# Typed graph convolution with residual and normalisation on one core: rank product behind the counts, register loads a step ahead, squares on ScalarE, edge codes on TensorE

## The chip, the cores and the metric

The kernel runs on one core of one Trainium2 chip. The metric is device time in microseconds of one execution; a profiled execution also gives a trace of every engine. Engines are named as the profile names them: PE (TensorE), PEld (its weight loads), DVE (VectorE), ACT (ScalarE), POOL (GpSimd) and SP (SyncE, which issues DMAs). A name with a q, such as DVEq, is the engine's sequencer.

## The reference

There are 12,500 nodes with 128 features and 400,000 edges, sorted by their target `dst`. Every edge is of one of two types.

```
Xs      = x[src]
m_data  = Xs @ W_data.T + b_data
m_ctrl  = Xs @ W_control.T + b_control
msg     = where(edge_type == 0, m_data, m_ctrl)
agg     = segment_sum(msg, dst, 12500)
h       = x + relu(agg + x @ W_self.T + b_self)
out     = (h - mean(h)) / sqrt(var(h) + 1e-5)      # over the 128 features
```

## The kernel before, in words

Sums commute with the products by W, so the kernel sums the rows of x by target and type first, and multiplies the sums by the weights after that. x is held as three bf16 parts of an fp32 number (`x3` in SBUF, `rows3` in DRAM), and one-hot matrices on TensorE pick and add rows.

The 400,000 edges are 25 groups (`g`, 125 chunks of 128 edges). A group has five windows; of each, 5 chunks are "p" chunks, whose rows come by an indirect DMA on POOL (`fetch`, tile `msg`, one gather per chunk), and 20 are "e" chunks, whose rows are picked from SBUF by matmuls (`pick`, tile `got`, cast by ACT to `emsg`). In two groups of three the fifth window consists of p chunks alone. That leaves 109 e windows, and the main loop has one step `w` for each. A step is five units `t` on PE: picks of some cells into `got`, then additions (`add`, into the bank `sums`, with the one-hot `esel` that DVE makes) of the cells picked one unit earlier. The last additions of a step are done in unit 0 of the next one, by `end`, which then has DVE add the bank to `acc` at an offset that a register holds (`accumulate`; `place_of` loads the register on DVE's queue, line 854). The p chunks go through banks of the same pair (`sums`, two buffers, `psel`), with counts in `cnt`.

Which edges go to which cell of a step is worked out by a chain on DVE, two steps ahead: `O` (the 0/1 matrix of edges and cells, made three steps ahead), `tens` and `fold_few` (its counts), `before` (four counting products on PE, line 634), `ahead` (a reduction of their result, line 642), `product` (O by ahead, line 648), `fold`, `eighth`, `found`, `rank`, `rank_matrix` (rm), `values` (rv). From rv PE makes the table (`put`, tile side, line 726), ACT casts it (`cell`), SP stores it and reads it back spread over all partitions (`pick`), and DVE compares it (`pick_matrix`). Edges beyond the table's room go a side way: `over` (a search for the 8 largest keys), `om_all` and line 574 on PE.

Two more jobs run beside the steps. `prep(g)` turns a group's indices and types into codes on the right partitions, by transposes on PE. `finish_batch`, 25 times, takes up to four tiles of finished sums, multiplies by the weights (line 1095), adds x, and normalises (`norm`, `write`).

PSUM holds one bank `side` (a single buffer, shared by put, the side way, prep, finish and before), two banks `sums`, and `got`. Each engine works its list strictly in order. The order is set by hand: every piece of work has a place between 0 and 1 in the step, `merged` sorts by it, and `in_turn` ties DVE's chain together; a scheduler then sets the final lists.

Of the kernel before, what the change touches and what calls it, by code (L numbers as in the profile page):

```python
# [8 lines left out]
FP = mybir.dt.float32  # L9
# [10 lines left out]
P = 128  # L20
# [188 lines left out]
def short_path(ctx, tc, const, ident, eps, wT, brow, bad, x, src, dst, etype, ws, bs, out):  # L209
# [269 lines left out]
    def prep(g):  # L479

        s, d, t = raw.pop(g)
        v = 0 if sets(g) == NE else 1
        width = bounds_of[:GC, v, 0:1]
        sf = pre.tile([GC, P], FP, name="sf", bufs=1)
        rel = pre.tile([GC, 2, P], BF, name="rel", bufs=1)
        code = pre.tile([GC, 2, P], FP, name="code_r", bufs=1)
        kind = pre.tile([GC, P], FP, name="kind_r", bufs=1)
        idx = pre.tile([P, GC], I32, name="idx_g", bufs=3)
# [6 lines left out]
        def rows():  # L495
            near = near_of(g, d)
            for k in range(2):
                nc.vector.tensor_scalar(rel[:, k], d, near[k], None, op0=OP.subtract)
            nc.vector.tensor_single_scalar(kind, t, 0.0, op=OP.not_equal)
            nc.vector.scalar_tensor_tensor(code[:, 1], kind, width, rel[:, 1], op0=OP.mult, op1=OP.add)  # L500
            nc.vector.scalar_tensor_tensor(code[:, 0], kind, float(PW), rel[:, 0], op0=OP.mult, op1=OP.add)
            for j, op in enumerate((OP.max, OP.min)):
                nc.vector.tensor_tensor(worst[:GC, v, j], worst[:GC, v, j], rel, op=op)

        def turn():
            ps = side()
            for k, each in enumerate((sf, code[:, 1], code[:, 0])):
                nc.tensor.transpose(ps[:, k * P:k * P + GC], each, ident[:GC, :GC])
# [86 lines left out]
    def give_slots(w):  # L595
# [32 lines left out]

        def before():
            s["ahead"] = side()  # L630
            cols = s["ahead"][:, :2 * NCELL].rearrange("p (k j) -> p k j", k=2)
            for a in range(4):
                cells = slice(a * NQ, (a + 1) * NQ)
                nc.tensor.matmul(  # L634
                    cols[:, :, cells], ltri[:, a, :], s["few"][:, 3 * CQ:3 * CQ + 2, cells],
                    start=(a == 0), stop=True, skip_group_check=True,
                )

        def ahead(prev=None):
            s["ahead_b"] = two.tile([P, NCELL], BF, name="ahead")  # L640
            with nc.allow_low_precision(reason="whole numbers; those over 256 need not be exact"), after(prev):
                return nc.vector.tensor_reduce(  # L642
                    s["ahead_b"], s["ahead"][:, :2 * NCELL].rearrange("p (k j) -> p j k", k=2), AX.X, OP.add
                )
# [201 lines left out]
    def acc_rows(g, a, b):  # L846
        begin_acc(g)
        return acc[g][:, a:b, :]

    def place_of(g, i):  # L850

        parts_in[g] = parts_in.get(g, 0) + 1
        with tc.issue_after(added[-2].ins) if len(added) > 1 else ExitStack():
            return nc.vector.value_load(raw["place"][0:1, g, i:i + 1], min_val=0, max_val=R - WMAX)  # L854
# [96 lines left out]

    def picked(w, tiled, ending, before):

# [46 lines left out]
        def unit(t):  # L1000
# [10 lines left out]
            if t == 0:  # L1011
                choose(0, 10)
                gates = ending() or [gate]
            while counts:
# [46 lines left out]
    def finish_batch(g, tiles):  # L1061
# [37 lines left out]
        def norm():  # L1099
            h = s["h"] = fp.tile([P, 4, D], FP, name="h")  # L1100
            st = fp.tile([P, 4, 6], FP, name="st")
            mv = s["mv"] = fp.tile([P, 4, 2], FP, name="mv")
            for i, (_, _, rows) in enumerate(tiles):
                nc.vector.scalar_tensor_tensor(
                    h[:rows, i, :], s["ph"][:rows, i * D:(i + 1) * D], 0.0, s["xs"][:rows, i, :], op0=OP.max, op1=OP.add
                )
            for i, (_, _, rows) in enumerate(tiles):
                if rows < full:
                    nc.vector.memset(mv[:, i, :], 1.0)
                nc.vector.bn_stats(st[:rows, i, :], h[:rows, i, :])  # L1110
                nc.vector.bn_aggr(mv[:rows, i, :], st[:rows, i, :])

        def write():
            h, mv = s["h"], s["mv"]
            rows = full
            sd = fp.tile([P, 4], FP, name="sd")
            nc.scalar.activation(sd[:rows, :k], mv[:rows, :k, 1], AF.Sqrt, bias=eps[:rows])
            rs = fp.tile([P, 4], FP, name="rs")
            nc.vector.reciprocal(rs[:rows, :k], sd[:rows, :k])
            for i, (n, _, r) in enumerate(tiles):  # L1120
                nc.vector.tensor_scalar(
                    h[:r, i, :], h[:r, i, :], mv[:r, i, 0:1], rs[:r, i:i + 1], op0=OP.subtract, op1=OP.mult
                )
# [95 lines left out]

    def ending():  # L1220
        pass

# [6 lines left out]
    for w in range(pairs):  # L1229
# [8 lines left out]
        if i == 3 and g + 2 < NG:  # L1238
            load(g + 2)
        tiled, begin, chain, first = {}, [], {}, None  # L1240
        if w + 2 < pairs:
            tiled, first, chain = slots[w + 2]["tiled"], slots[w + 2]["before"], slots[w + 2]["chain"]
            begin = [(0.58, slots[w + 2]["over"])]
        elif w + 2 == pairs:
            tiled, begin = last_spares()
            first = begin.pop(0)[1]
        if w + 3 < pairs:
            more += [(0.503, lambda: begin_slots(w + 3))]
# [4 lines left out]
        units, ending, (second, third) = picked(w, tiled, ending, first)  # L1253
# [4 lines left out]
        order = [  # L1258
            (0.305, second), (0.31, chain.get("ahead")), (0.33, chain.get("product")), (0.34, chain.get("half")),
            (0.36, third), (0.38, chain.get("fourth")), (0.51, chain.get("eighth")),  # L1260
            (0.52, chain.get("found")), (0.53, started("same")), (0.54, chain.get("rank")),
            (0.55, chain.get("matrix")), (0.56, chain.get("key")), (0.57, chain.get("values")),
            (0.6, (lambda prev: pick_matrix(w + 1, prev)) if w + 1 < pairs else None),
            (0.62, started("blocks")), (0.64, started("tens")), (0.66, started("fold5")),
            (0.67, started("fold2")), (0.68, started("fold1")),
        ]
# [163 lines left out]
```

## Time and profile before

| | us |
|---|---|
| median of 3 runs | 1719.48 (1718.93 to 1721.28) |
| the profiled execution's own time | 1719.45 |
| its span | 1717.7 |
| busy: DVE | 1577.5 |
| busy: PE | 1554.5 |
| busy: ACT | 1229.1 |
| busy: POOL | 1217.5 |

Busy times are unions of instruction times, without register, semaphore and DMA-issuing instructions. The granted clock of PE was 0.996. An engine's idle time is put down to what it waited for last; "issue" stands where the profile shows nothing to wait for. In rows of groups, the numbers behind the bar are the busy time, the mean duration in ns, and the idle time ahead of the group with what ended it.

### The profile page before, as it was taken

The page shows a single profiled execution, that of the slowest core. Times are in us where ns is not written, and L with a number is a line of the kernel's source. Part 1 is how long each engine was busy: PE and PEld are TensorE (multiplying, and loading weights), DVE is VectorE, ACT ScalarE, POOL GpSimd, SP SyncE. Part 2 cuts the span into 40 slices and gives each one's busy share as a digit, 9 for nine tenths or more (in the row PEclk, how much of TensorE's full clock was granted, in tenths as well). Part 3 has the DMA queues.
Part 4 walks back from the last instruction along what each step waited for, and adds up shares of the span by engine and source line. Part 5 has one row for each costly group of instructions (what it writes and reads, how often), then busy time and mean ns, then how long its engine had stood idle before and what let it go on. Part 6 is the DMA issues. An engine that isn't in the chain of part 4 may idle for free.

```text
span 1717.7 us, 67684 instructions
## 1 busy us (share of the span) xinstructions
PE 1554.5 (90%) x27966; PEld 1225.1 (71%) x27966; DVE 1577.5 (92%) x4078; ACT 1229.1 (72%) x2056; POOL 1217.5 (71%) x1022
## 2 busy tenths in 40 slices
PE   0699999899999999899899999999999999999998
PEld 0477777777777777777777777777777777777776
DVE  9799999999999999999999999999999999999994
ACT  7677767677767777677676777677686777677774
POOL 1377767777776777667777777677777787787682
PEclk9999999999999999999999999999999999999999
DMA  7944444444454444444444454444444454444442
GB/s 227 269 136 134 148 129 148 135 150 135 133 153 133 146 151 132 148 130 140 143 140 135 137 157 132 148 152 132 142 133 150 139 156 130 128 148 129 141 125 59
DMA packets 147605, 246.05 MB, mean 143 GB/s; under 512 B 35565, under 2 KB 114264, under 8 KB 147288
## 3 DMA queue, kind: packets, MB, share of 16 engines
q1 hardware_dynamic: 99128, 142.50, 24.9%
q0 software_dynamic: 48160, 99.14, 21.8%
q8 instruction: 221, 3.62, 0.8%
q14 instruction: 96, 0.79, 0.1%
HBM read 224.04 MB, written 17.52 MB: 141 GB/s over the span
## 4 chain that ended last, share of the span: by engine, by line
DVE 66%; PE 19%; issue 7%; ACT 3%; DVEq 3%; DMA 1%; SPq 0%; ACTq 0%
DVE esel L541 9%; PE sums L803 8%; DVE O L541 6%; DVE prod L656 6%; PE got L974 6%; DVE pick L790 5%; DVE prod L648 5%; DVE rv L713 4%; DVE psel L541 3%; DVE prod L627 3%; DVE prod L622 3%; DVE rm L541 2%; DVEq L854 2%; DVE found L666 2%; DVE prod L612 2%
## 5 line engine op out<-in xcount | busy, mean ns | idle before, releaser
L871 POOL DMA_INDIRECT msg<-rows,idx_g x945 | 1140.2, 1207 | 365.3 <-PE got L974 121.0
L988 ACT CAST emsg<-got 128x768 bf16<-128x768 f32 x1090 | 965.5, 929 | 305.0 <-PE got L974 291.2
L803 PE MATMUL sums<-esel,emsg 128*128 128x172 bf16 x7848 | 685.9, 238 | 7.9 <-DVE acc L860 7.8
L803 PEld LDWEIGHTS <-emsg 128*128 128x128 bf16 x7848 | 571.2, 98 | 118.8 <-issue 111.7
L974 PE MATMUL got<-x,pick 128*32 128x384 bf16 x10682 | 578.9, 330 | 9.8 <-ACT emsg L988 3.8
L974 PEld LDWEIGHTS <-pick 128*32 128x32 bf16 x10682 | 246.5, 96 | 138.3 <-issue 19.8
L541 DVE TENSOR_TENSOR esel<-code_col,code 128x1720 bf16<-128x1720 bf16 x327 | 293.5, 897 | 18.1 <-issue 12.9
L803 PE MATMUL sums<-psel,msg 128*128 128x48 bf16 x2835 | 161.4, 183 | 17.6 <-DVE acc L860 17.3
L803 PEld LDWEIGHTS <-msg 128*128 128x128 bf16 x2835 | 134.1, 97 | 26.2 <-issue 24.7
L648 DVE TENSOR_TENSOR prod<-O,ahead 128x2000 bf16<-128x2000 bf16 x109 | 130.9, 1201 | 9.9 <-DVE ahead L642 5.1
L656 DVE TENSOR_TENSOR prod<-prod 128x1200 bf16<-128x1200 bf16 x218 | 135.8, 623 | 3.0 <-DVE prod L648 0.2
L541 DVE TENSOR_TENSOR O<-cell_col,blk 128x2000 bf16<-128x2000 bf16 x109 | 129.7, 1190 | 0.5 <-ACT blk L443 0.5
L947 POOL DMA_INDIRECT both<-rows,idx x55 | 72.2, 1313 | 78.4 <-ACT emsg L988 37.1
L726 PE MATMUL side<-rv,O 128*128 128x64 bf16 x2180 | 84.8, 195 | 38.2 <-DVE rv L713 29.9
L790 DVE TENSOR_SCALAR pick<-pick,lane_f 128x3200 bf16<-128x3200 bf16 x109 | 112.5, 1033 | 1.5 <-DMA pick<-there 1.5
L726 PEld LDWEIGHTS <-O 128*128 128x128 bf16 x2180 | 81.0, 100 | 44.2 <-DVE rv L713 24.1
L541 DVE TENSOR_TENSOR psel<-near_col,near 128x1200 bf16<-128x1200 bf16 x125 | 96.4, 771 | 6.4 <-issue 6.3
L627 DVE TENSOR_TENSOR prod<-prod 128x500 bf16<-128x500 bf16 x327 | 94.1, 288 | 3.3 <-DVE prod L627 1.8
L713 DVE TENSOR_TENSOR rv<-rm,vals 128x1280 bf16<-128x1280 bf16 x109 | 89.5, 821 | 0.0
L622 DVE TENSOR_TENSOR prod<-O 128x1000 bf16<-128x1000 bf16 x109 | 72.9, 669 | 0.1
L860 DVE TENSOR_TENSOR acc<-acc,sums 128x172 f32 (+2 forms) x234 | 65.6, 280 | 6.3 <-PE got L974 1.6
L642 DVE TENSOR_REDUCE ahead<-side 128x100 bf16<-128x200 f32 x109 | 39.2, 360 | 30.0 <-PE side L634 27.8
(197 smaller groups left out, 1522.1 us busy)
## 6 DMA issues: line engine op xcount, KB each, us to landing
pick<-there SPq DMA_DIRECT2D x108, 800.0 KB
msg<-rows,idx_g POOLq DMA_INDIRECT x945
acc<-acc_start SPq DMA_DIRECT2D x23, 640.0 KB
rows<-x SPq DMA_DIRECT2D x6, 1344.0 KB
xs<-in_x_dram SPq DMA_DIRECT2D x99, 62.5 KB
out_dram<-h SPq DMA_DIRECT2D x99, 62.5 KB
xt<-in_x_dram SPq DMA_DIRECT2D x6, 896.0 KB
cnt<-cnt_start SPq DMA_DIRECT2D x22, 160.0 KB
```

The source lines that it names most:

```text
L541: ins = nc.vector.tensor_tensor(sel.rearrange("p n (w t) -> p n w t", t=2), col[:rows].rearrange("p (o w t) -> p o w t", o=1, t=2).to_broa ...
L622: return nc.vector.tensor_add(h[:, :2 * CQ], s["O"][:, :2 * CQ], s["O"][:, 2 * CQ:])
L627: return nc.vector.tensor_add(h[:, to:to + n], h[:, a:a + n], h[:, b:b + n])
L648: return nc.vector.tensor_tensor(s["prod"][:, :, :NCELL], s["O"], s["ahead_b"].rearrange("p (o j) -> p o j", o=1).to_broadcast([P, EC, NCE ...
L656: return nc.vector.tensor_add(prod[:, :, :h], prod[:, :, :h], prod[:, :, h:2 * h])
L713: placed[:] = [nc.vector.tensor_tensor(rv.rearrange("p c v (r t) -> p c v r t", t=2), s["rm"].rearrange("p c (o r t) -> p c o r t", o=1, t ...
L726: nc.tensor.matmul(s["rk"][:m, :2 * CAP], s["held"][:, c * NCELL:c * NCELL + m], s["rv"][:, c].rearrange("p v r -> p (v r)"), start=(c == ...
L790: return nc.vector.tensor_scalar(t, t, lane_f, None, op0=OP.is_equal)
L803: last = nc.tensor.matmul(out, msg[:, j * D:(j + 1) * D], sel, start=(start and j == 0), stop=stop, skip_group_check=True)
L871: return nc.gpsimd.indirect_dma_start(out=msg, out_offset=None, in_=rows3[:, :], in_offset=bass.IndirectOffsetOnAxis(ap=codes["p", g][0][: ...
L974: last = nc.tensor.matmul(ps[CAP * a:CAP * (a + 1), :], slots[w]["pick"][:, a * NQ + q, :], x3[:, 4 * q + a - a0].rearrange("p j d -> p (j ...
L988: s["out"] = nc.scalar.copy(msg[:, :n], ps[:, :n, :3 * D])
```

## The change

Five things change.

- **The counting products** of w+2 (`before`) move from unit 1 of a step to the end of the previous step's additions in unit 0. They write to free columns of that step's `sums` bank instead of a `side` bank of their own. `ahead` and `product` follow directly on DVE, and the rest of the chain, the selections and the work for w+3 get new, even places from 0.21 to 0.69. `over` moves from 0.58 to 0.7, the making of the slots for w+3 from 0.503 to 0.2.
- **The registers** for the next step's places are loaded within DVE's chain, one behind `product` and the others behind `O`, and kept until they are used.
- **The variance**: the two statistics instructions per tile go. The instruction that makes h also writes the row's sum; one small instruction scales it; ACT squares the difference with a running sum, into the buffer of x, and the root takes it with a factor 1/128.
- **The edge codes**: type times width plus distance is no longer made by two DVE instructions and turned by fp32 transposes, but by two accumulating bf16 products each, with the identity and with an identity times the width (`type_step`, made once).
- **The types' flags** (`kind`) are bf16.

```diff
+    type_step = keep.tile([P, 3, P], BF, name="type_step")
+    for v in range(2):
+        nc.vector.tensor_scalar(type_step[:, v], ident_b, bounds_of[:, v, 0:1], None, op0=OP.mult)
+    nc.vector.tensor_scalar(type_step[:, 2], ident_b, float(PW), None, op0=OP.mult)
...
-            nc.vector.scalar_tensor_tensor(code[:, 1], kind, width, rel[:, 1], op0=OP.mult, op1=OP.add)
-            nc.vector.scalar_tensor_tensor(code[:, 0], kind, float(PW), rel[:, 0], op0=OP.mult, op1=OP.add)
...
-            for k, each in enumerate((sf, code[:, 1], code[:, 0])):
-                nc.tensor.transpose(ps[:, k * P:k * P + GC], each, ident[:GC, :GC])
+            nc.tensor.transpose(ps[:, :GC], sf, ident[:GC, :GC])
+            for k, of in ((1, v), (0, 2)):
+                turned = ps[:, (2 - k) * P:(2 - k) * P + GC]
+                for j, (each, scale) in enumerate(((rel[:, k], ident_b), (kind, type_step[:, of]))):
+                    nc.tensor.matmul(
+                        turned, each, scale[:GC, :GC], start=(j == 0), stop=(j == 1), skip_group_check=True
+                    )
...
-        def before():
-            s["ahead"] = side()
-            cols = s["ahead"][:, :2 * NCELL].rearrange("p (k j) -> p k j", k=2)
+        def before(bank=None):
+            begins = bank is None
+            s["ahead"] = side()[:, :2 * NCELL] if begins else bank[:, 2 * EW:2 * EW + 2 * NCELL]
+            cols = s["ahead"].rearrange("p (k j) -> p k j", k=2)
...
+    def load_place(prev, w, k):
+
+        needed = [(gp, 2 * ip) for gp, ip in (divmod(p, NE) for p in closed.get(w, []))]
+        gp, ip = each_e[w - 1]
+        needed.append((gp, 2 * ip + 1))
+        for gp, ip in needed[k:] if k else needed[:1]:
+            with after(prev):
+                places[gp, ip] = nc.vector.value_load(
+                    raw["place"][0:1, gp, ip:ip + 1], min_val=0, max_val=R - WMAX
+                )
+        return prev
...
-        def end():
+        def end(counted=None):
...
             for u in more:
                 u()
+            if counted:
+                counted(s["ps"])
             accumulate(place_of(g, 2 * i + 1), acc_rows(g, 0, 2), s["ps"], EW, EW)
...
+                nc.vector.scalar_tensor_tensor(
+                    h[:rows, i, :], s["ph"][:rows, i * D:(i + 1) * D], 0.0, s["xs"][:rows, i, :],
+                    op0=OP.max, op1=OP.add, accum_out=mv[:rows, 0, i:i + 1],
+                )
+            nc.vector.tensor_scalar(mv[:full, 0, :k], mv[:full, 0, :k], -1.0 / D, None, op0=OP.mult)
+            for i, (_, _, rows) in enumerate(tiles):
+                nc.scalar.activation(
+                    s["xs"][:rows, i, :], h[:rows, i, :], AF.Square, bias=mv[:rows, 0, i:i + 1],
+                    accum_out=mv[:rows, 1, i:i + 1],
+                )
...
-            (0.305, second), (0.31, chain.get("ahead")), (0.33, chain.get("product")), (0.34, chain.get("half")),
...
+            (0.21, chain.get("ahead")),
+            (0.234, chain.get("product")),
+            (0.258, (lambda prev: load_place(prev, w + 1, 0)) if w + 1 < pairs else None),
+            (0.282, second),
...
```

The lists of the engines show the moves at three places. First DVE, at the begin of a step in which a group is passed on (`cnt` and `acc` are added to the next group's). TENSOR_LOAD and the ISA rows behind it are a register load; esel of 1548 columns is `second`. Before:

```order
L854 TENSOR_LOAD place_i
L854 ISA x2
L840 TENSOR_TENSOR cnt<-cnt 128x140
L541 TENSOR_TENSOR esel<-code_col,code 128x1548
L860 ISA
L860 TENSOR_TENSOR acc<-acc,sums 128x2x86
...
L839 TENSOR_TENSOR acc<-acc 128x2x140
L642 TENSOR_REDUCE ahead<-side 128x100
L854 TENSOR_LOAD place_i
L854 ISA x2
L648 TENSOR_TENSOR prod<-O,ahead 128x20x100
```

Now:

```order
L846 TENSOR_TENSOR cnt<-cnt 128x140
...
L882 ISA
L882 TENSOR_TENSOR acc<-acc,sums 128x2x86
L648 TENSOR_REDUCE ahead<-sums 128x100
L845 TENSOR_TENSOR acc<-acc 128x2x140
L654 TENSOR_TENSOR prod<-O,ahead 128x20x100
L865 TENSOR_LOAD place_i
L865 ISA x2
L546 TENSOR_TENSOR esel<-code_col,code 128x1548
```

The loads stand behind the product, the selection too, and the reduction directly behind the addition to acc.

Second PE, around the counting products of a plain step: `got` is a pick, `sums<-esel` an addition. Before:

```order
L974 LDWEIGHTS pick
L974 MATMUL got_20214<-x_104,pick 32x384
L634 LDWEIGHTS ltri
L634 MATMUL side<-prod,ltri 128x2x25
...
L803 LDWEIGHTS emsg_20100
L803 MATMUL sums<-esel,emsg_20100 128x172
```

Now:

```order
L809 LDWEIGHTS last
L809 MATMUL sums<-esel,last 128x172
L640 LDWEIGHTS ltri
L640 MATMUL sums<-prod,ltri 128x2x25
...
L924 LDWEIGHTS one_col
L924 MATMUL sums<-psel,one_col 32x120
```

The four products stood behind the picks of unit 1 and now stand behind the last additions (`last` holds the rows of the side way) of the previous step.

Third ACT, in a step with a finishing batch: `cell` is the cast of put's result, `sd` the root. Before:

```order
L988 CAST emsg_20472<-got_20471 128x768
L988 CAST emsg_20485<-got_20484 128x1152
L734 CAST cell<-side 128x64
L702 CAST bits_b<-bits 128x48
L988 CAST emsg_20564<-got_20563 128x768
L1117 ACTIVATE sd<-mv,eps 125x4
```

Now:

```order
L1010 CAST emsg_20410<-got_20409 128x1152
L1010 CAST emsg_20480<-got_20479 128x768
L1135 ACTIVATE xs,mv<-h,mv 125x128 x4
L740 CAST cell<-side 128x64
L1144 ACTIVATE sd<-mv,eps 125x4
L1010 CAST emsg_20493<-got_20492 128x1152
```

Four squares stand ahead of cell, and the root follows cell directly.

More of the change, by code (lines that the diff above doesn't have):

```diff
@@ L482, in prep @@
         v = 0 if sets(g) == NE else 1
-        width = bounds_of[:GC, v, 0:1]
         sf = pre.tile([GC, P], FP, name="sf", bufs=1)
         rel = pre.tile([GC, 2, P], BF, name="rel", bufs=1)
-        code = pre.tile([GC, 2, P], FP, name="code_r", bufs=1)
-        kind = pre.tile([GC, P], FP, name="kind_r", bufs=1)
+        kind = pre.tile([GC, P], BF, name="kind_r", bufs=1)
         idx = pre.tile([P, GC], I32, name="idx_g", bufs=3)
@@ L950, in spare_rows, with picked @@
         )
-    def picked(w, tiled, ending, before):
+    def picked(w, tiled, ending, before, counted):
         g, i = each_e[w]
```

61 lines of the change are left out of this document (34 added, 27 removed).

## Prediction

> **What bounds the kernel now.** I read the page's busy times first, then the chain that ended last, then the stretch between start and end.
>
> ```profile
> span 1717.7 us, 67684 instructions
> PE 1554.5 (90%) x27966; PEld 1225.1 (71%) x27966; DVE 1577.5 (92%) x4078; ACT 1229.1 (72%) x2056; POOL 1217.5 (71%) x1022
> DVE 66%; PE 19%; issue 7%; ACT 3%; DVEq 3%; DMA 1%; SPq 0%; ACTq 0%
> 80.00:1680.00 1600.00, 1496.96 (x27220) 1182.22 (x27216) 1496.88 (x3815) 1158.01 (x1966) 1196.69 (x985) 1.00 0.47 140
> ```
>
> The columns of the stretch are PE, PEld, DVE, ACT and POOL, busy us and instructions. In the 1600 us from 80 to 1680 DVE is busy 1496.9 us and PE 1497.0: each idles 103 us. The chain runs through DVE for two thirds, so DVE comes first and PE close behind. The 118 us outside are start and end, which the change hardly touches. The sum is made against the profiled execution, 1719.45 us (1.75 over its span); the median of the runs shown, 1719.48, is the same.
>
> So the question is which of DVE's idle and which of its work goes. Its waits, longest first, and two of PE's and one of ACT's:
>
> ```profile
> DVE ahead L642 <- PE side L634: 27.8, 45, 2.5
> DVE esel L541 <- issue: 12.9, 35, 0.9
> DVE psel L541 <- issue: 6.3, 13, 1.6
> DVE prod L648 <- DVE ahead L642: 5.1, 13, 0.7
> DVE rs L1119 <- ACT sd L1117: 4.8, 11, 0.9
> DVE cnt L840 <- issue: 4.6, 14, 0.5
> PE side L574 <- DVE om_all L568: 31.6, 38, 1.6
> PE sums L803 <- DVE acc L860: 25.1, 39, 1.2
> ACT emsg L988 <- PE got L974: 291.2, 368, 6.7
> ```
>
> **Register loads.** "Issue" is a wait for nothing the profile names. The chain at one such place, and the load's own rows:
>
> ```profile
> 811.60 0.09 DVE rank L671
> 811.69 0.17 DVEq L854
> 811.92 0.40 issue
> 812.32 1.05 DVE esel L541
> L854 DVEq TENSOR_LOAD <-place_i x234: 298/304/1396, 55.7 to 1705.0; - x117
> L854 DVEq FUSED_REGOPS  x234: 183/190/206, 56.9 to 1705.4; - x117
> L648 DVE TENSOR_TENSOR prod<-O,ahead 128x2000 bf16<-128x2000 bf16 x109 | 130.9, 1201 | 9.9 <-DVE ahead L642 5.1 <-issue 2.3
> L541 DVE TENSOR_TENSOR O<-cell_col,blk 128x2000 bf16<-128x2000 bf16 x109 | 129.7, 1190 | 0.5 <-ACT blk L443 0.5
> ```
>
> A load holds DVE's queue for 304 + 190 ns and some gaps, about 0.6 us, and the engine runs dry when the instruction ahead of it is short. The three issue rows above and that of the product (a load stands between it and ahead) make 12.9 + 6.3 + 5.1 + 4.6 = 28.9 us. The changed kernel loads as often, but behind the product (1201 ns) or the cell matrix O (1190 ns), which outlast 0.6 us; two loads in a row, some 20 times, show perhaps 0.2 us each. So -29 + 4 = **-25**. Ends: -29 (all hidden) and -12 (half of that comes back). The product and O are the whole cover: ahead of them a load would show its 0.4 us again.
>
> **Rank product behind the counts, in the sums bank.** The counting products (four matmuls) move from behind the next step's picks to directly behind the last additions of the step; the reduction "ahead" follows acc on DVE. A selection (esel, 958 ns) that stood before acc now stands behind the product.
>
> ```profile
> L541 DVE TENSOR_TENSOR esel<-code_col,code 128x1548 bf16<-128x1548 bf16 x109 | 104.4, 958 | 10.9 <-issue 8.2 <-PE got L974 2.1 <-PE sums L803 0.5
> L541 DVE TENSOR_TENSOR psel<-near_col,near 128x1200 bf16<-128x1200 bf16 x125 | 96.4, 771 | 6.4 <-issue 6.3
> ```
>
> The wait that goes is ahead's 27.8 us. What is late next is acc, which waits for PE's additions and is reached 0.9 us sooner. PE has 25.1 us of waits on acc at the bank, and the bank is now held through the reduction too; but acc comes sooner by about as much. I take half of the 27.8: **-14**; ends -28 and 0. The transfer of work on PE is nil: the same four matmuls. On PE, om_all's 31.6 us should shrink, since the selection no longer stands near it; I count it in the sum, not here. The early start of w+3's slots and the later top-8 search issue no DMA; the gathers on POOL keep their gates on PE and come as much sooner as PE does, and on SP the store and broadcast of pick follow cell, so the next step's picks gain that time too.
>
> **Edge codes on TensorE.** Two DVE instructions per group of 25 go, each in its stream about 80 ns shorter than its duration (the rows of the next part show it: a 0.25 us instruction at 819.70, the next at 819.87).
>
> ```profile
> L500 DVE SCALAR_TENSOR_TENSOR code_r<-kind_r,bounds_of,rel 125x128 f32<-125x128 f32 x25 | 8.8, 352 | 0.0
> L501 DVE SCALAR_TENSOR_TENSOR code_r<-kind_r,rel 125x128 f32<-125x128 f32 x25 | 7.0, 279 | 0.0
> ```
>
> 25 x (0.27 + 0.20) = **-12**; ends -12 and -6 (if PE is what the step waits for). PE swaps two fp32 transposes per group for four bf16 products of the same width: I take 0 there, between -5 and +5 us for 25 groups. Three small table instructions at the start lie beside the fetch of x.
>
> **Squares on ScalarE.** One batch of four tiles before, DVE, then PE's put and ACT's casts beside it:
>
> ```profile
> 819.02 0.28 DVE L1104 SCALAR_TENSOR_TENSOR h<-side,xs 125x128 f32<-125x128 f32 x1
> 819.22 0.47 DVE L1110 BATCH_NORM_STATS2 st<-h 125x6 f32<-125x128 f32 x2
> 819.70 0.25 DVE L1110 BATCH_NORM_STATS2 st<-h 125x6 f32<-125x128 f32 x1
> 819.87 0.16 DVE L1111 BATCH_NORM_AGGREGATE mv<-st 125x2 f32<-125x6 f32 x1
> 820.21 0.24 DVE L860 TENSOR_TENSOR cnt<-cnt,sums 64x120 f32 x1
> 820.38 0.16 DVE L1111 BATCH_NORM_AGGREGATE mv<-st 125x2 f32<-125x6 f32 x1
> 820.47 0.20 DVE L860 TENSOR_TENSOR acc<-acc,sums 128x80 f32 x1
> 821.96 0.17 DVE L1119 RECIPROCAL rs<-sd 125x4 f32<-125x4 f32 x1
> 819.35 0.76 PE L726 MATMUL side<-rv,O 128*128 128x64 bf16 x20 [1.35 <-DVE h L1104]
> 820.15 0.21 ACT L734 CAST cell<-side 128x64 bf16<-128x64 f32 x1 [2.13 <-PE side L726]
> L493 ACT CAST sf<-srcs 125x128 f32<-125x128 int32 x25 | 7.4, 296 | 4.7 <-PE side L508 2.8 <-DMA srcs<-in_src_dram 0.8
> L842 ACT ACTIVATION_READ_ACCUMULATOR spill<-cnt,most 64x1 f32 x24 | 4.5, 188 | 0.0
> ```
>
> From 819.22 to 820.47 less the count's 0.17 is 1.08 us of statistics; 101 tiles are 25 such batches: -27. Added on DVE: a small scaling per batch, 0.09 in the stream, +2; and the running sum inside 101 instructions. No row shows that on DVE. Ends: nothing, and 101 x 0.188 (ACT's read of its sum) = 19; I take 0.09 each, the stream share of the shortest rows here, +9.
>
> The Trainium skill ("VectorE: DVE Perf Modes", Two Vector instructions with no wait between them) counts an instruction with an accumulator output as two, the second a read of the accumulator. By that rule, at ACT's 188 ns, the total would come out 10 us above mine; with no second instruction, 9 below. No DVE row here shows it.
>
> On ACT 101 squares are added, by the two ACT rows between 0.28 and 0.48 us each; I take 0.40. ACT has 291 us of waiting for picks to hold those 40 us. But the squares now stand ahead of cell and of the root sd. Counted from the last sum instruction's end: mean ready at +0.3, squares to +1.9, cell and sd to +2.3. DVE reaches the reciprocal at +1.2 where only acc and one 771 ns selection lie between, in 8 batches; in 2 only a selection lies between, in 2 nothing; elsewhere parts of the next group or the product cover it. 10 x 1.1 + 2 x 2 = 15, less the 4.8 waited now: +10. Together -27 + 2 + 9 + 10 = **-6**; ends -30 and +44 (19 for the sums, 50 if every batch waits 2 us). Behind the reciprocal on DVE stand om_all, four normalisations and acc, so PE waits with it.
>
> **The sum.** -25 - 14 - 12 - 6 = -57. PE has to give up as much: of its 103 us of idle the two waits above, 31.6 + 25.1 = 57, are for a late DVE, which a lighter and reordered DVE ends. So PE can follow, just, and I take no more: 1719.45 - 57 = **1662**.
>
> **Rivals.**
> 1. All covers hold and PE yields as much: loads -29, ahead -28, codes -12, squares -16 (the reciprocal waits no longer than now, +9 - 27 + 2), -85, 1634. For it: the longest waits of PE name DVE. Against it: PE would be left with 18 of its 103 us of idle.
> 2. PE holds: half of DVE's 57 turns into waits at acc, -29, 1690. For it: PE is as busy as DVE. Against it: the same two waits.
> 3. POOL becomes the bound.
>
> ```profile
> L871 POOL DMA_INDIRECT msg<-rows,idx_g x945 | 1140.2, 1207 | 365.3 <-PE got L974 121.0 <-issue 117.3 <-PE sums L803 98.3
> 786.01 1.66 POOL L871 DMA_INDIRECT msg<-rows,idx_g  x1 [0.30 <-PE side L726]
> 792.65 1.13 POOL L871 DMA_INDIRECT msg<-rows,idx_g  x1 [0.30 <-issue]
> ```
>
> In the stretch POOL is busy 1196.7 us with 985 instructions, and 0.30 us lies ahead of each: 1492 of 1600. At my forecast it has 1543, so it does not bind; if a gather with its gap went from 1.51 to 1.60 us it would need 1576, and the time were 1719 - 24 = 1695. The Trainium skill ("SBUF — State Buffer", Who interferes with whom) says that DVE in its two-port modes locks GpSimd out of a shared port, and so its descriptors. The spread from 1.13 to 1.66 us agrees, and a denser DVE would by that rule lengthen gathers.
>
> 4. Every saving comes back as a wait, acc standing for PE where ahead and the loads stood before: within 1716 to 1723. Against it: 29 us of loads and 39 of codes and statistics (12 + 27) are DVE's own, not PE's.
> 5. Slower: the reciprocal. ACT's order puts cell, which needs PE's put, ahead of sd; where put comes 2 us later than at 819.35, sd ends past +4.3 and DVE stands 3 us and more. Without the 10 us that I counted the sum is -67; 25 waits above 2.8 us make it slower. At 3.9 us: -67 + 97, 1749. Against it: put started right behind the sums' release here, and DVE waited 4.8 us in all.
>
> **Chances.** Forecast (1645 to 1680) 0.47; rival 1 0.18; rival 2 0.15; rival 3 0.06; rival 4 0.05; rival 5 0.09. A measurement of this kernel can tell 0.2%, 3.4 us, from no change. Faster 0.47 + 0.18 + 0.15 + 0.06 = 0.86, same 0.05, slower 0.09. The range 1630 to 1704 takes in rivals 1 to 3 and leaves out some 2 in 10: rivals 4 and 5, and the tails of rivals 1 and 3. The terms' ends add to -29 - 28 - 12 - 30 = -99 and -12 - 0 - 6 + 44 = +26, and POOL's 1492 forbids gains beyond 108.
>
> **What would show it.** Right: the four issue and load waits on DVE under 10 us in all; the waits of ahead under 15; no statistics and no code_r groups, the sum instructions (0.28 us at 819.02) at 0.28 to 0.40 us; squares of 0.3 to 0.45 us on ACT; waits of the reciprocal on sd of 10 to 20; om_all waits on PE well under 31.6. Wrong: issue waits that stay behind the product or O; acc waiting for PE by 20 us and more; the reciprocal waiting above 40 us; gathers above 1.3 us mean with PE waiting for a DMA of msg.

## The result and the profile after

The changed kernel takes 1746.6 us (median of 4 runs, 1737.6 to 1754.0), the kernel before 1720.4 beside it: 1.015 times as long, 95% interval 1.010 to 1.020. The forecast was 1662. The profiled execution took 1737.64 us.

Later comparisons fell on chips of two kinds, and each ratio below is against the kernel before on the same chip. On the first kind the kernel before takes 1720 us (the runs above, e7, e8, e9, e16), on the second 1943 to 1967 (all others); what differs there is told with the last experiments.

The page of the changed kernel: span, busy times, and the engines' shares of the chain that ended last; then the stretch from 80 to 1680 us, with the columns of the prediction's.

```profile
span 1735.7 us, 67730 instructions
PE 1577.4 (91%) x28016; PEld 1234.5 (71%) x28016; DVE 1529.9 (88%) x3956; ACT 1264.8 (73%) x2258; POOL 1307.5 (75%) x1022
PE 44%; DVE 26%; DMA 11%; ACT 9%; issue 7%; DVEq 1%; POOL 1%; SPq 0%; ACTq 0%; POOLq 0%
80.00:1680.00 1600.00, 1505.90 (x27044) 1181.21 (x27036) 1442.38 (x3665) 1180.23 (x2133) 1274.42 (x976) 0.99 0.47 139
```

DVE is busy 48 us less (1577.5 to 1529.9) and is no longer where most of the chain runs (66% to 26%). But POOL has 90 us more (1217.5 to 1307.5) with the same 1022 instructions. With 0.30 us ahead of each, POOL needs 1274.4 + 976 x 0.30 = 1567 us of 1600, where it needed 1492. Its gathers and the waits say how that came:

```profile
L893 POOL DMA_INDIRECT msg<-rows,idx_g x945 | 1234.2, 1306 | 306.5 <-issue 141.1
ACT last L1054 <- DMA both<-rows,idx: 75.7, 23, 10.0
PE sums L809 <- ACT last L1054: 48.0, 15, 8.5
DVE acc L882 <- PE sums L640: 79.5, 55, 8.6
DVE rs L1146 <- ACT sd L1144: 31.1, 21, 3.2
DVE esel L546 <- issue: 3.8, 9, 0.9
DVE ahead L648 <- PE side L640: 3.7, 2, 3.2
PE side L579 <- DVE om_all L573: 1.8, 2, 1.0
PE sums L809 <- DVE acc L882: 3.0, 9, 0.7
PE side L567 <- DVE over_n L699: 21.7, 31, 1.7
```

The waits that the change was to end are gone: esel for the register loads (12.9 to 3.8), ahead (27.8 to 3.7), PE for om_all (31.6 to 1.8) and for acc (25.1 to 3.0). In their place stands a chain that the kernel before doesn't show at all: ACT waits 75.7 us for `both`, the rows of the side way, which a gather fetches through the same list on POOL as msg; PE waits for ACT's copy of them (`last`), and acc on DVE for PE. Once in full, from the timeline:

```profile
1039.13 0.95 POOL L969 DMA_INDIRECT both<-rows,idx  x1 [0.30 <-issue]
1044.76 0.51 ACT L1054 COPY last<-both 64x384 bf16<-64x384 bf16 x1 [10.03 <-DMA both<-rows,idx]
1045.33 0.61 PE L809 MATMUL sums<-esel,last 128*128 128x172 bf16 x3 [8.53 <-ACT last L1054]
1046.15 0.33 DVE L882 TENSOR_TENSOR acc<-acc,sums 128x172 f32 x1 [8.57 <-PE sums L640]
1040.00:1045.00 5.00, 0.00 (x0) 0.00 (x0) 0.00 (x0) 0.24 (x1) 3.78 (x5) 0.50 0.63 226
1045.00:1050.00 5.00, 4.67 (x47) 3.38 (x48) 3.81 (x6) 3.99 (x6) 3.78 (x5) 0.50 0.30 78
```

ACT stands from 1034.7 on; the gather starts only at 1039.13, without a wait of its own (0.30 us behind the one ahead: POOL was behind). So it was with nearly all: of the 23 late gathers of `both`, 21 stood at the end of a row of 19 to 168 POOL instructions with at most 0.33 us between them. PE loses 8.5 us. The last two rows, windows of 5 us, show the granted clock at 0.50, first while PE stands and then for 5 us of its work; from 1050 to 1055 it is 0.98. The Trainium skill ("TensorE: Matmul & The Clock Gate", Part 1) says that PE's clock is halved after an idle window of some 3.4 us and comes back after a busy one; the trace agrees (PE stood from 1036.8 to 1045.33, at a clock of 0.50 from 1040 on). Not every late `both` costs clock: in five of the 23 cases PE stood for 5 us and more. From 80 to 1680 us the granted clock was under 0.9 for 48 us, 32 of them with PE at work; in the kernel before for 3.4 us. By an estimate from these figures, 32 us of work at half clock cost some 16 us; PE's waits for ACT's copy are 48.

In the kernel before, the same gather and copy in one step:

```profile
795.50 0.95 POOL L947 DMA_INDIRECT both<-rows,idx  x1 [0.30 <-ACT idx_g L509]
801.64 0.51 ACT L1032 COPY last<-both 64x384 bf16<-64x384 bf16 x1
```

The copy comes 5.2 us behind the end of the gather and waits for nothing.

Why do the gathers last longer? POOL and DVE beside each other in the changed kernel:

```profile
1224.41 6.15 POOL L893 DMA_INDIRECT msg<-rows,idx_g  x1 [0.30 <-PE got L996]
1224.82 1.19 DVE L654 TENSOR_TENSOR prod<-O,ahead 128x2000 bf16<-128x2000 bf16 x1
1225.93 0.95 DVE L546 TENSOR_TENSOR esel<-code_col,code 128x1548 bf16<-128x1548 bf16 x1
1226.81 0.77 DVE L662 TENSOR_TENSOR prod<-prod 128x1200 bf16<-128x1200 bf16 x1
1227.50 0.68 DVE L546 TENSOR_TENSOR esel<-code_col,code 128x1032 bf16<-128x1032 bf16 x1
1228.11 0.46 DVE L662 TENSOR_TENSOR prod<-prod 128x600 bf16<-128x600 bf16 x1
1228.49 1.04 DVE L546 TENSOR_TENSOR esel<-code_col,code 128x1720 bf16<-128x1720 bf16 x1
1229.45 0.29 DVE L667 TENSOR_TENSOR prod<-prod 128x280 bf16<-128x280 bf16 x1
1229.78 0.48 DVE L672 TENSOR_REDUCE found<-prod 128x20 f32<-128x320 bf16 x1
```

The seven TENSOR_TENSOR instructions, each with two bf16 inputs in SBUF, overlap each other by some 0.08 us, since each is independent of the one just ahead. The first gap is at 1229.74, where found needs the result of the fold ahead of it, and the gather ends at 1230.56, 0.82 us behind it. In the kernel before the fold stood directly behind the product, which it reads:

```profile
806.48 1.20 DVE L648 TENSOR_TENSOR prod<-O,ahead 128x2000 bf16<-128x2000 bf16 x1
806.97 1.53 POOL L871 DMA_INDIRECT msg<-rows,idx_g  x1 [0.30 <-PE side L1078]
807.72 0.79 DVE L656 TENSOR_TENSOR prod<-prod 128x1200 bf16<-128x1200 bf16 x1
```

Here the gap begins at 807.68, and the gather ends at 808.50, 0.82 us later.

In the changed kernel 31 gathers lasted over 3 us (3 before). They make the whole rise of the mean: without them it is 1196 ns, and 1200 before without its three. A gap is not needed to free a gather. 28 of the 31 ended 0.79 to 0.85 us behind the end of a TENSOR_TENSOR with both inputs in SBUF whose next DVE instruction either starts behind a gap (16 of them) or reads at most one tensor from SBUF, without any gap (such as found, or acc and cnt, whose other input is the bank in PSUM). An instant picked at random lies so in 3.8% of cases. The other three ended 0.12 us behind the end of pick, which follows such a row. Pick, a TENSOR_SCALAR with one input, holds gathers too: 63 of the 945 gathers before and 52 in the changed kernel end 0.11 to 0.13 us behind a pick, where chance would give one.

### The profile page after: what moved, and what is told of

Same layout as the page of the kernel before. It is cut to its first block, busy times and chain, and to the rows that moved or that the text cites. A ratio compares the mean times of both kernels' runs of the same rounds, so it can differ in the third digit from the quotient of the medians.

```text
span 1735.7 us, 67730 instructions
## 1 busy us (share of the span) xinstructions
PE 1577.4 (91%) x28016; PEld 1234.5 (71%) x28016; DVE 1529.9 (88%) x3956; ACT 1264.8 (73%) x2258; POOL 1307.5 (75%) x1022
## 4 chain that ended last, share of the span: by engine, by line
PE 44%; DVE 26%; DMA 11%; ACT 9%; issue 7%; DVEq 1%; POOL 1%; SPq 0%; ACTq 0%; POOLq 0%
PE sums L809 20%; PE got L996 14%; DVE esel L546 5%; ACT emsg L1010 4%; DMA both<-rows,idx 4%; PE side L1119 4%; DMA msg<-rows,idx_g 3%; DVE O L546 3%; DMA pick<-there 3%; DVE pick L796 2%; DVE prod L662 2%; ACT xs L1135 2%; DVEq L865 1%; DVE prod L632 1%; PE sums L924 1%
## 5 line engine op out<-in xcount | busy, mean ns | idle before, releaser
L893 POOL DMA_INDIRECT msg<-rows,idx_g x945 | 1234.2, 1306 | 306.5 <-issue 141.1
L809 PE MATMUL sums<-esel,emsg 128*128 128x172 bf16 x7848 | 696.6, 239 | 1.2 <-ACT emsg L1010 0.8
L996 PE MATMUL got<-x,pick 128*32 128x384 bf16 x10682 | 600.4, 332 | 16.8 <-ACT emsg L1010 11.0
L969 POOL DMA_INDIRECT both<-rows,idx x55 | 68.3, 1241 | 64.4 <-DMA dsts<-in_dst_dram 27.8
L732 PEld LDWEIGHTS <-O 128*128 128x128 bf16 x2180 | 80.1, 100 | 31.6 <-DVE rv L719 26.6
L1054 ACT COPY last<-both 64x384 bf16<-64x384 bf16 x54 | 27.5, 509 | 75.8 <-DMA both<-rows,idx 75.7
```

The source lines that it names most:

```text
L732: nc.tensor.matmul(s["rk"][:m, :2 * CAP], s["held"][:, c * NCELL:c * NCELL + m], s["rv"][:, c].rearrange("p v r -> p (v r)"), start=(c == ...
L809: last = nc.tensor.matmul(out, msg[:, j * D:(j + 1) * D], sel, start=(start and j == 0), stop=stop, skip_group_check=True)
L893: return nc.gpsimd.indirect_dma_start(out=msg, out_offset=None, in_=rows3[:, :], in_offset=bass.IndirectOffsetOnAxis(ap=codes["p", g][0][: ...
L996: last = nc.tensor.matmul(ps[CAP * a:CAP * (a + 1), :], slots[w]["pick"][:, a * NQ + q, :], x3[:, 4 * q + a - a0].rearrange("p j d -> p (j ...
```

## The experiments

Theory A: the denser order of DVE holds POOL's gathers, POOL's list fills, and `both` comes late. Theory B: the squares on ScalarE cost the time. Theory C: the counting products in the sums bank do.

**The changed kernel once more (e7).**

> The changed kernel itself, unchanged, as the measure for e1 to e6, which ran on chips where the kernel before took 1943 to 1964 us. Where the kernel before takes near 1720, it should take 1740 to 1750 with POOL without a gap for long stretches (as many as 168 gathers in a row ahead of one 'both'). On a chip like those of e1 to e6, theory A expects no such stretches (POOL waits for PE there) and a time 3 to 5% above the kernel before, since e1_chain was 2.5% and e2_statistics_back 5.5% above; theory B expects it above e2_statistics_back, 5.5% and more; theory C likewise 3 to 5%.

On a chip of the first kind: 1742.5 us, 1.013 (1.009 to 1.017) of the kernel before. Its gathers last 1299 ns and ACT waits 71.7 us for `both`, 24 times. The result is not an accident of one chip.

**Fewer gathers (e3, e6, e9; in the kernel before e4).** Every 8th gather of msg is left out, 118 of 945; its chunk adds the message before it, so that PE, DVE and ACT do the same work and the sums are not the reference's.

```diff
+    fetched_all = []
 
     def fetch():
         g, i, c = to_fetch.pop(0)
+        if len(fetched_all) % 8 == 7:
+            fetched_all.append(None)
+            fetched.append([m for m in fetched_all if m is not None][-1])
+            return None
...
+        fetched_all.append(msg)
...
```

> The kernel of e3 and e6 once more (every 8th gather of msg left out of the changed kernel). Theory A, on a chip like that of e7: POOL gets gaps again, ACT's wait for 'both' falls from 72 us to under 15, and the time to 1650 to 1680. Theories B and C: 1735 to 1755.

On a chip of the first kind: 1663.9 us (1662.2 to 1668.2), 0.968 (0.966 to 0.970) of the kernel before.

```profile
L899 POOL DMA_INDIRECT msg<-rows,idx_g x827 | 1093.7, 1323 | 339.8 <-PE got L1004 128.3
ACT last L1062 <- DMA both<-rows,idx: 5.4, 8, 0.9
DVE acc L882 <- PE sums L640: 31.0, 48, 1.8
DVE rs L1154 <- ACT sd L1152: 31.5, 21, 3.2
80.00:1680.00 1600.00, 1530.17 (x27706) 1206.25 (x27698) 1462.25 (x3747) 1210.24 (x2194) 1164.48 (x873) 1.00 0.45 134
```

The gathers are as long as ever (1323 ns), but POOL needs 1164.5 + 873 x 0.30 = 1426 us of 1600, `both` is in time, and 80 us are gone. So with room in POOL's list the stall ends. Theory B falls as the main cause, since the squares and the 31.5 us of waiting for the root are all still there. Theory C keeps 31 us of acc's wait (1.2 in the kernel before), no more. By itself e9 leaves one rival, which the expectation of e4 names: that leaving gathers out helps whatever the order of DVE. e4 was not run on the first kind; the runs with gaps, which leave out nothing, bear on it below.

The same two edits on chips of the second kind:

> The changed kernel with every 8th gather of msg left out (its chunk uses the message before it), 118 of 945; nothing else is changed. POOL has 118 x 1.6 = 190 us less to do. Theory A: POOL's list has room, 'both' is in time, and the time falls to what the other engines allow, 1650 to 1680. Theories B and C: POOL does not bind, 1735 to 1755.

> The kernel before with every 8th gather of msg left out in the same way, 118 of 945. POOL had room there (1492 of 1600 us in the stretch), so all theories expect little: 1705 to 1722. A fall as large as in the changed kernel would say that leaving gathers out helps whatever the order of DVE, by taking work from PE's gates or from the shared port.

> The same kernel as e3_fewer_gathers, every 8th gather of msg left out of the changed kernel, on another chip for the same reason. Theory A: POOL's list has room (1573 of 1600 us less some 170), ACT's wait for 'both' falls from 76 us to under 15, 1650 to 1680. Theories B and C: 1735 to 1755.

e3: 0.998 (0.996 to 1.000); e6: 0.994 (0.991 to 0.996); e4: 0.956 (0.952 to 0.960). All miss: e3 and e6 were to fall to 1650 to 1680 by theory A, and no theory expected e4 to gain. On this kind of chip e4's rival is what came out.

**The chain's folds in a row (e1, e5, e8).**

```diff
-            (0.282, second),
-            (0.306, chain.get("half")),
-            (0.33, third),
-            (0.354, chain.get("fourth")),
-            (0.378, chain.get("eighth")),
-            (0.402, chain.get("found")),
+            (0.282, chain.get("half")),
+            (0.306, chain.get("fourth")),
+            (0.33, chain.get("eighth")),
+            (0.354, chain.get("found")),
+            (0.378, second),
+            (0.402, third),
```

> The kernel of e1 and e5 once more; on the chip of e7 the kernel before took 1720.7 us, the changed kernel 1742.5, and ACT waited 72 us for the rows of the side way ('both'). Theory A, on such a chip: with the folds and the search in a row and the two selections behind them, gathers last 1250 ns or less at the mean (1306 in the changed kernel), ACT's wait for 'both' falls under 30 us, and the time to 1660 to 1700. Theories B and C: gathers may change, but the time stays at 1735 to 1755.

On a chip of the first kind: 1714.3 us (1707.4 to 1718.4), 0.996 (0.994 to 0.998).

```profile
L893 POOL DMA_INDIRECT msg<-rows,idx_g x945 | 1206.8, 1277 | 307.1 <-issue 144.8
ACT last L1054 <- DMA both<-rows,idx: 48.3, 17, 6.8
554.37 4.40 POOL L893 DMA_INDIRECT msg<-rows,idx_g  x1 [0.30 <-issue]
555.91 1.05 DVE L546 TENSOR_TENSOR esel<-code_col,code 128x1720 bf16<-128x1720 bf16 x1
556.87 0.82 DVE L719 TENSOR_TENSOR rv<-rm,vals 128x1280 bf16<-128x1280 bf16 x1
557.61 1.05 DVE L796 TENSOR_SCALAR pick<-pick,lane_f 128x3200 bf16<-128x3200 bf16 x1
```

Less than expected: gathers lose 29 ns instead of 56, and 30 of the 80 us come back. The direction is theory A's (B and C expected no change of the time). The timeline suggests why it is half: the selections now make a new row without a gap with rv, pick and O. The gather shown ends 0.11 us behind pick, as 73 of the 945 do here (52 in the changed kernel). The next runs break up this row too.

> Theory A (POOL): in the changed kernel DVE runs product, two selections and three folds without a gap, gathers on POOL last longer under such a train (mean 1306 ns for 1207), POOL's list fills up (1573 of 1600 us with its gaps), the gather of the rows of the side way ('both') comes late, and with it ACT's copy 'last', PE's additions and DVE's acc (waits of 76, 48 and 80 us). Here the folds, the top-8 and its search stand in a row, each waiting for the one before, and the two selections behind them, so that gaps come back: gathers 1250 ns or less, ACT's wait for 'both' under 30 us, time 1660 to 1700. Theory B (squares) expects no change in these waits and 1735 to 1755. Theory C (counting products in the bank: acc waits for PE because PE has them there) expects acc to wait for PE as long as now, near 80 us, and 1735 to 1755.

> The same kernel as e1_chain, on another chip: on the one of e1 to e4 the kernel before took 1963.6 us, and results of PE reached ACT late (the cast of put's result 0.83 us at the median behind the start of the last product, 0.25 in the first profiles), so that POOL was not what bound there. Theory A, where the kernel before takes near 1720: gathers 1250 ns or less at the mean, ACT's wait for 'both' under 30 us, 1660 to 1700. Theory B (squares) and theory C (counting products): no change against the changed kernel, 1735 to 1755.

On the second kind e1 took 1.025 (1.019 to 1.030) and e5 1.022 (1.019 to 1.024) of the kernel before, which misses theory A's times; gathers 1230 and 1228 ns.

**Gaps everywhere (e10, e14, e16).** The same instructions; only the places from 0.282 to 0.546 in the chain change.

```diff
...
+            (0.282, chain.get("half")),
+            (0.306, chain.get("fourth")),
+            (0.33, second),
+            (0.354, chain.get("eighth")),
+            (0.378, chain.get("found")),
+            (0.402, chain.get("rank")),
+            (0.426, third),
+            (0.45, chain.get("matrix")),
+            (0.474, chain.get("values")),
+            (0.498, (lambda prev: pick_matrix(w + 1, prev)) if w + 1 < pairs else None),
+            (0.522, chain.get("key")),
+            (0.546, started("same")),
             (0.57, started("blocks")),
```

> The kernel of e10 and e14 once more, both of which fell on chips where the kernel before takes 1944 to 1961 us. Where it takes 1720, theory A: gathers of 1200 ns or less at the mean, ACT's wait for 'both' under 15 us, 1650 to 1690. If only the amount of work on DVE counts, not its gaps: gathers of 1277 ns as in e8_chain, 1705 to 1720.

On a chip of the first kind: 1684.8 us (1681.8 to 1687.1), 0.979 (0.977 to 0.981) of the kernel before.

```profile
L893 POOL DMA_INDIRECT msg<-rows,idx_g x945 | 1152.4, 1219 | 326.3 <-issue 130.4
ACT last L1054 <- DMA both<-rows,idx: 5.8, 5, 2.5
DVE acc L882 <- PE sums L640: 29.1, 41, 1.8
DVE rs L1146 <- ACT sd L1144: 24.1, 22, 3.4
80.00:1680.00 1600.00, 1534.97 (x27712) 1211.25 (x27701) 1475.29 (x3748) 1209.70 (x2194) 1211.18 (x991) 1.00 0.48 141
```

As theory A expected (1650 to 1690), with gathers of 1219 ns slightly above its 1200. With not one instruction more or fewer on any engine, some 60 us go, ACT's wait falls from 75.7 to 5.8 us, only 6 gathers last over 3 us, and the kernel beats both the changed one and the one before. No gather is left out here, so e4's rival cannot account for these 60 us; for the 21 us between this kernel and e9 it stays open. The new order cuts the rows by gaps and by instructions of another kind alike, and no run tells the two apart. The four runs side by side:

| kernel | mean gather, ns | ACT's wait for `both`, us | time, us |
|---|---|---|---|
| changed | 1306 | 75.7 | 1746.6 |
| folds in a row (e8) | 1277 | 48.3 | 1714.3 |
| gaps (e16) | 1219 | 5.8 | 1684.8 |
| fewer gathers (e9) | 1323 | 5.4 | 1663.9 |

> Theory A, sharpened by the traces so far: a gather that starts under DVE instructions on two-byte operands ends 0.82 us behind the first gap of 0.034 us between two of them (where the later one reads what the one just ahead of it wrote), or behind an instruction of another kind. In e8_chain a row without such a gap was left: selection, rv, pick, O (4 us). Here no row in the chain is longer than 1.9 us: half and fourth stand behind the product, one selection behind them, the search next, one selection behind rank, rv behind rm, and key and same between pick and O. Theory A: gathers of 1200 ns or less at the mean, ACT's wait for 'both' under 15 us, 1650 to 1690. If only the amount of work on DVE counts, and not its gaps: gathers as in e8_chain (1277), 1705 to 1720.

> The kernel of e10 once more: that chip was again of the kind on which the kernel before takes 1943 to 1964 us and PE's results come late (only they: ACT's and DVE's results arrive as fast as ever). There its gathers lasted 1202 ns (1248 and 1250 in e2 and e11, with the changed kernel's order), as theory A has it, but POOL had room anyhow. Where the kernel before takes 1720, theory A: gathers of 1200 ns or less, ACT's wait for 'both' under 15 us, 1650 to 1690. If only the amount of work on DVE counts: as e8_chain, 1705 to 1720.

On the second kind e10 took 1.019 (1.014 to 1.024) and e14 1.020 (1.015 to 1.024) of the kernel before, with gathers of 1202 ns: the effect on the gathers is there, the gain against the kernel before is not.

**The statistics on DVE again (e2, e11; with gaps e13, e18).** The two statistics instructions of the kernel before, no squares.

```diff
...
-                nc.scalar.activation(
-                    s["xs"][:rows, i, :], h[:rows, i, :], AF.Square, bias=mv[:rows, 0, i:i + 1],
-                    accum_out=mv[:rows, 1, i:i + 1],
-                )
+                nc.vector.bn_stats(st[:rows, i, :], h[:rows, i, :])
+                nc.vector.bn_aggr(mv[:rows, i, :], st[:rows, i, :])
...
```

> The changed kernel with the two statistics instructions on DVE and no squares on ScalarE. Theory A: the train of selections and folds is untouched, gathers stay near 1300 ns and the time within 1725 to 1750. Theory B (the squares cost the time: the reciprocal waits 31 us for the root, cell stands behind the squares): the waits for the root go, and the time falls by 30 us or more, to 1700 to 1715. Theory C: 1735 to 1755.

> The kernel of e2 (statistics on DVE again, no squares) on a chip where the kernel before takes near 1720. Theory A: POOL is as full as in the changed kernel, 1725 to 1750; the wait of the reciprocal falls from 31 us to 10 or less without the time following it. Theory B: 1700 to 1715.

> The order of e10 with the statistics on DVE again. It prices the squares where POOL doesn't bind. My own terms (27 us of statistics less 2 and 9, less 10 of waiting) say 5 us slower than e10. By the traces since (accumulator reads of 8 us, 27 us of waiting for the root) the two ways cost about the same: within 10 us of e10.

> The order of e16 (1684.8 us) with the statistics on DVE again, as e13. It prices the squares where POOL doesn't bind. The prediction's terms (27 us of statistics less 2 and 9, less 10 of waiting) say 1691. By what the traces show since (reads of the sum 8 us, 24 us of waiting for the root in e16) the two ways cost about the same, 1675 to 1695. Theory B (the squares cost the time) says below 1670.

All four fell on the second kind of chip: e2 1.055 (1.050 to 1.059) and e11 1.054 (1.048 to 1.060) in the changed kernel's order, slower than any theory expected (the changed kernel itself was not run on this kind, so that is no price of the squares); e13 1.021 (1.016 to 1.027) and e18 1.016 (1.011 to 1.021) in the order with gaps. The last two bracket e10 and e14, so there the squares cost and save nothing that can be told. On the first kind their price was not measured.

**More gathers in the kernel before (e12, e15, e17).** One more behind every 8th, into a tile that nothing reads.

```diff
+            extra.append(gather)
+            if len(extra) % 8 == 0:
+                g, i, c = to_fetch[0] if to_fetch else (NG - 1, NE - 1, 0)
+                again = mp.tile([P, 3 * D], BF, name="again", bufs=1)
+                nc.gpsimd.indirect_dma_start(
+                    out=again, out_offset=None, in_=rows3[:, :],
+                    in_offset=bass.IndirectOffsetOnAxis(ap=codes["p", g][0][:, i * CHUNKS + c:i * CHUNKS + c + 1], axis=0),
+                )
```

> The kernel before with one more gather behind every 8th of msg, into a tile that nothing reads: 118 more. Its POOL needed 1492 of 1600 us with the gaps; 118 x 1.51 = 178 more make 1670. Theory A: POOL becomes the bound there too, 'both' comes late and ACT waits for it by 50 us and more, the time is 1775 to 1830. If POOL's load is hidden (theories B and C): 1715 to 1735.

> The kernel of e12 once more (118 more gathers in the kernel before), where the kernel before takes 1720 us. Theory A: POOL's list needs 1670 of 1600 us, 'both' comes late, ACT waits for it by 50 us and more, 1775 to 1830. Theories B and C: 1715 to 1735.

> The kernel of e12 and e15 (118 more gathers in the kernel before), where the kernel before takes 1720 us. Theory A: POOL's list needs 1670 of 1600 us, 'both' comes late, ACT waits for it by 50 us and more, 1775 to 1830. If POOL's load were hidden: 1715 to 1735.

All three on the second kind: 1.090 (1.086 to 1.094), 1.089 (1.084 to 1.094), 1.088 (1.080 to 1.095). The time went up by some 170 us, but not in the way that theory A said: ACT's wait for `both` in e12 is 6.0 us, not 50 and more. Whether POOL's load alone makes the kernel before stall on the first kind stays untested.

**What the second kind of chip shows.** There the kernel before takes 220 to 250 us longer. DVE and ACT are as busy as on the first kind (1550.7 and 1268.7 us in e10, 1541.3 and 1264.0 in e16, the same kernel), PE is 124 us busier (1686.7 and 1562.6). Two rows of waits and the shares of the chain, from e10:

```profile
PE 66%; ACT 17%; issue 8%; DVE 4%; another core or an unknown queue 2%; DMA 2%; ACTq 0%; SPq 0%; DVEq 0%; POOL 0%
ACT emsg L1010 <- remote: 49.3, 19, 6.0
ACT emsg L1010 <- PE sums L809: 116.8, 81, 4.1
```

PE's results reach the others late: from the start of put's last product to ACT's cast of it the median is 1.26 us in e10 and 0.25 in e16. The trace names no cause. There each gather costs time though POOL waits for PE: 118 fewer saved 4.4%, 118 more cost 9%. Why is open; these runs say nothing on what bounds the kernel on the first kind, where the forecast was made.

## Why the prediction was wrong

**The step that failed** stands behind rival 3: "At my forecast it has 1543, so it does not bind." It priced POOL's room with the gather of the kernel before, 1.207 us. The change made the gather 1.306; with 0.30 ahead 1.61, and 985 instructions need 1582 us, more than the 1543. The rival named that very number (1.60), gave it a chance of 0.06, and a price of 1695, too low by 52 us: it took POOL's mean, and left out that `both` stands in the same list, so that a late gather stops ACT's copy, PE and acc, and at times halves PE's clock. Of the sign named for it, the gathers above 1.3 us came, but not PE waiting for msg (1.4 us): ACT waited for `both`. That rival 5's price, 1749, lies near the measured time is luck; its wait is not the cause.

The rows to see it stood beside the two gathers that the prediction shows, on DVE:

```profile
785.66 1.19 DVE L541 TENSOR_TENSOR O<-cell_col,blk 128x2000 bf16<-128x2000 bf16 x1
791.76 1.20 DVE L648 TENSOR_TENSOR prod<-O,ahead 128x2000 bf16<-128x2000 bf16 x1
```

The gather of 786.01 ended at 787.67, 0.82 us behind O; that of 792.65 at 793.78, 0.82 us behind the product. The prediction read the order of DVE only for what waits there, and put the spread of the gathers down to two-port modes. The Trainium skill ("SBUF — State Buffer", Who interferes with whom) has `tensor_tensor` in no two-port mode, but says that a DVE instruction with two inputs in SBUF contends with a GpSimd instruction that reads SBUF. The trace agrees: a gather reads its list of rows from SBUF, and rows of just such instructions held one for 6.15 us. The same section infers that they leave GpSimd's making of descriptors alone; these gathers were held all the same, and the measurement decides.

**Register loads: right.** Four waits under 10 us were forecast; they are 3.8 for esel, 0.6 for cnt, none for psel and the product.

**Rank product: the wait moved.** ahead's wait went (27.8 to 3.7), but where POOL does not bind acc waits 29 to 31 us for PE, just behind the counting products (1.2 before), above the 20 us that were named as a sign of being wrong. So the term of -14 came out at about +5: DVE reaches the bank sooner, PE does not.

**Edge codes: as written.** The two groups are gone, and PE and DVE show no wait in their place. They were not taken alone.

**Squares: mis-sized.**

```profile
L1129 DVE SCALAR_TENSOR_TENSOR h<-side,xs 125x128 f32<-125x128 f32 (+2 forms) x101 | 26.0, 280 | 13.4 <-PE side L1119 13.4
L1129 DVE DVE_READ_ACCUMULATOR h<-side,xs 125x1 f32 (+2 forms) x101 | 8.1, 80 | 0.0
L1135 ACT ACTIVATE xs<-h,mv 125x128 f32<-125x128 f32 (+2 forms) x101 | 39.5, 402 | 5.0 <-DVE mv L1133 4.8
```

The running sum costs 8.1 us (9 forecast; the Trainium skill's second instruction, "VectorE: DVE Perf Modes", Two Vector instructions with no wait between them, is there, at 80 ns), the squares 402 ns (400). But the reciprocal waits 31.1 us for the root, where 15 was forecast and 10 to 20 named as the sign of being right. So -27 + 2 + 8 + 26 = +9 in place of -6. Rival 5 named this wait, but at 31 us it does not decide: e9 holds it and is fast.

**PE can follow: right.** om_all and acc cost PE 4.8 us in place of 57; 16.5 of it came back at over_n (5.2 us in the list of before, 21.7 now), since the search stands later in the step. With POOL's room restored (e9) the time is 1663.9, where 1662 was forecast. That agreement is luck: e9 makes 118 gathers fewer than the kernel that was forecast, and the terms do not agree. Rank product and squares gave nothing, and what made up for them was not taken apart. With all gathers the best time is e16's, 1684.8.

## What to carry to other kernels

Before taking work off a busy engine or packing it closer, ask what used its gaps: here gathers on another engine did, and a DVE that was busy 48 us less came with a kernel 26 us slower. Price the next bound with the durations that it will have beside the new order, not with those of the old, and look at which urgent transfer shares its queue. Where selections are to be spread through a chain, cut long rows of instructions with two inputs in SBUF, by leaving instructions that need each other's results side by side or, as the ends of the gathers suggest, by putting a short one with at most one input in SBUF between: the same work in another order was worth 60 us.

## What was not expected of the hardware

Rows of DVE instructions with two bf16 inputs in SBUF that follow one another without a gap stretched a gather on POOL from 0.95 us to 6.15 us. It ended 0.82 us behind the first pause, of 0.034 us, between two instructions; other gathers ended as far behind the first instruction that reads at most one tensor from SBUF (28 of the 31 longest one way or the other). Pick, a TENSOR_SCALAR of 1.05 us, held gathers until 0.12 us behind its end. In a pause of 8.5 us on PE the granted clock fell to 0.50 and stayed there for the first 5 us of work behind it. And chips differ: on one kind the kernel before takes 1720 us, on the other 1943 to 1967, with PE's results late for no cause that the trace shows, and an order that wins 2.1% on the one loses 2% on the other.
